# Reordered expert tiles, mask additions and ending in a fused attention and mixture-of-experts block

## The chip, the cores and the metric

The kernel runs on one core of a Trainium2 chip. The metric is the device time of one launch in microseconds (us). The core has five engines that run side by side, each with an instruction stream of its own: TensorE (PE) for matrix products, VectorE (DVE), ScalarE (ACT) and GpSimd (POOL) for the rest of the arithmetic, and SyncE (SP), which here only issues transfers. The engines wait for one another through semaphores. Data lies in SBUF (128 partitions); products are accumulated in PSUM.

## The reference

The input `query` has 2048 rows of 512. With xn = layernorm(query), the output is query + attention(xn) + experts(xn), all in float32.

```python
# attention: 16 heads, each with two score maps of width 16
q, k = rotary(xn @ Wq), rotary(xn @ Wk)
v = xn @ Wv                                    # 16 heads of 32
a1 = softmax(causal(q1 @ k1.T * 16 ** -0.5)) @ v
a2 = softmax(causal(q2 @ k2.T * 16 ** -0.5)) @ v
d = irfft((rfft(a1) - lam * rfft(a2)) * filt)  # along time, filt a Gaussian
attention = rmsnorm(d, over=32) * rms_weight * (1 - LAMBDA_INIT) @ Wout
# experts: 8 of inner width 352, the top 2 of each row; one shared of 704
s, e = top2(softmax(xn @ gate.T)); s = s / sum(s)
routed = sum_k s_k * ((silu(xn @ w1[e_k]) * (xn @ w3[e_k])) @ w2[e_k])
experts = routed + (silu(xn @ sw1) * (xn @ sw3)) @ sw2
```

## The kernel before

The rows are 16 tiles of 128 (`NT`), in 4 chunks of 512 (`QC`). Heads are worked in 8 pairs g. The order of PE, DVE, ACT, POOL and, in the middle part, SP is that in which the program issues instructions (`manual_schedule`).

**Start, up to about 250 us.** Layer norm, values, router, the list of slots for the routed rows, and the projections of queries and keys, which go out to memory.

**Middle, to about 1241 us.** The list `stream` holds the attention as 544 units: for each pair g and chunk qc from 3 down to 0, blocks of keys `kb`. A unit's `scores` (L822) puts transposed scores in PSUM, ACT takes the exponential into a tile `pt` (L835), and in the diagonal blocks POOL zeroes what lies beyond the diagonal with an `affine_select` (L840). Units with such blocks are called masked. `values` (L862) multiplies `pt` with v on PE, and `added` adds `pt` into `sum` on DVE (L876, L879). When a chunk is complete, `sums` (L888), `finish` (L900 to L908: `rcp`, `o_n`) and `put` (L917) turn it into the normalised difference in `vd`. When a pair is complete, `folded` (L928 to L970) does the sixteen-tile part of the filter's Fourier transform; POOL takes it in steps between other work, and the last pair is folded on DVE.

Between the attention units runs the generator `experts()`. It first does the shared expert for tiles that were left, then 34 tiles (`NR`) of routed rows. The first 28 (`NP`) hold 128 rows of one expert; each of the last 6 holds 64 rows of each of two experts. One tile goes through `xh` and `xg` (L180: products with the up weights `wu`), `xtanh` (DVE L191, L197), a transpose `ps_u` (PE L206) and its copies `uT` (DVE L208, L209), `xy` (L216: product with the down weights `wd`), `y_sb` (ACT L225) and a store to the array `ys` (SP L228). The weights have two buffers, `w_sb[0]` and `w_sb[1]`, each with a `wu` of 1408 KB and a `wd` of 768 KB. A single-expert tile uses one of them, a two-expert tile both. SP fetches `wu` (L146) into a buffer when `xg` has left it, and `wd` (L149) after `xy`. These stand behind the loads of queries `qS` and keys `kS` (L739) and the stores of `ys` in SP's queue. The rows of a tile, `xrow`, come by an indirect transfer that POOL issues (L623). PSUM tiles of `xh`, `xg`, `xy`, `ps_sum`, `ps_u`, `ps_ot`, `ps_st` share a pool of three buffers.

The units are taken in groups of four. A group issues the scores of its first two, the values of the group before, `sums` of a closing chunk, the other two scores, `finish`, and then the additions and one or more pieces of `experts()`:

```python
added(before)
added(u for u in units[:2] if not masked(u))
later = [u for u in units[2:] if not masked(u)]
while True:
    work()
    ...
added(later)
added(u for u in units if masked(u))
```

**Ending, from about 1241 us.** The shared expert of the last tile (`kept`; products `wh` L246 through the function `several`, its gate `ws` on ACT L256 and DVE L257 to L263), the convolution products of the filter (`ps_r`, `ps_z`, L1141), and then eight pairs of tiles: `y` (L1163), squares (ACT L1219), means (L1223, L1224), scale `a` (L1234), transposes `ps_tr` (L1262), the projection `po` (L1270), the addition to the residual `res` (L1275) and the store (L1276). `Pair`, `prepared`, `across`, `projected` and `finished` are these steps. Beside it, `res` is put together: SP loads 12 of the 16 tiles of `query` (L1120), POOL adds the shared expert's rows to them (L1123) and two gathers of `ys` (L1125), each a transfer that accumulates; the last four tiles follow in `still`, when buffers come free.

Of the kernel before, what the change touches and what calls it, by code (L numbers as in the profile page):

```python
# [8 lines left out]
F32 = mybir.dt.float32  # L9
# [4 lines left out]
ALU = mybir.AluOpType  # L14
# [31 lines left out]
NR = NS - 2  # L46

NP = (T * TOP // HALF - NX) // 2
WUP = NE * 2 * FI
WCOL = WUP + NF * E  # L50
CONVS = 23
# [16 lines left out]
def block_kernel(  # L68
# [527 lines left out]
    def middle(general):  # L596


        with ExitStack() as pools:
# [29 lines left out]
            def experts():  # L629
# [7 lines left out]
                for t0 in range(EARLY, NT - 1, TQ):  # L637
                    t1 = min(t0 + TQ, NT - 1)
                    last = t1 == NT - 1
                    cols = slice(t0 * P, t1 * P)  # L640
                    for n, us in enumerate(chunks(xnT[:, :, cols], u_last)):
                        if last and n == 0:
                            who_sb = mp.tile([P, E], F32, tag="x", name="who_sb")
                            who_sb = who_sb[:NR].rearrange("n (k p o) -> n k p o", k=TOP, o=2)
                            for k in range(TOP):
                                nc.sync.dma_start(who_sb[:, k], who[k][: NR * P, :].rearrange("(n p) o -> n p o", p=P))
                        elif last and n == 2:
                            nc.vector.tensor_add(who_sb[:, 0], who_sb[:, 0], who_sb[:, 1])
                        elif last and n == 3:
                            ps = bank([P, 2, NR], "ps_w")  # L650
                            for i in range(2):
                                nc.tensor.transpose(ps[:, i, :], who_sb[:, 0, :, i], ident[:NR, :NR])
                            nc.vector.tensor_copy(tok, ps[:, 0, :])
                            nc.vector.tensor_copy(wcol, ps[:, 1, :])
                        elif last and n == 5:


                            xr = [rows_of(0), rows_of(1)]
                            es = [routed(0)]
                            fetch_up(es[0], 0, nc.sync)  # L660
                        yield 3.45 * (t1 - t0) / TQ
                    if last:
                        es.append(routed(2))
                        fetch_up(es[1], 1, nc.sync)
                    for t in range(t0, t1):
                        y = result(us, t - t0, range(NF))
                        yield 2.6
                        stored(result(us, t - t0, range(NF, SCH), y), ysh[t], 0.5)
                        yield 2.6
# [5 lines left out]
                xT, late = transposed(xr.pop(0)), None  # L675
                yield 0.6

                sets = [[j] if j < NP else [2 * j - NP, 2 * j - NP + 1] for j in range(NR)]
                halves = [2 * j + i for j in range(NR) for i in range(len(sets[j]))]

                def places(j, part):
                    return [w_sb[n % 2][part] for n in sets[j]]

                def tile_down(j, uT):
                    return places(j, 1), uT, ys[j * P : (j + 1) * P, :], wcol[:, j : j + 1]

                for j in range(NR):
                    if j > 0:
                        late = tile_down(j - 1, turned_back(u))
                    half = up_first(places(j, 0), xT)  # L690
                    yield 2.9 if late else 2.4
                    u = up_third(places(j, 0), xT, half)
                    if j + 2 < NR:
                        xr.append(rows_of(j + 2))
                    for n in sets[j]:

                        m = n + 2 - len(halves)
                        es.append(routed(halves[n + 2]) if m < 0 else wex[NX + m : NX + m + 1])
                        fetch_up(es[n + 2], n % 2, nc.sync)
                    yield 2.4  # L700
                    if j + 1 < NR:
                        xT = transposed(xr.pop(0))
                    if late:
                        down(*late)
                        for n in sets[j - 1]:
                            fetch_down(es[n + 2], n % 2, nc.sync)
                    if j == 1:
                        shared.append(True)
                    if late:
                        yield 3.2  # L710
# [46 lines left out]
            def greatest(g, qc):  # L757
# [28 lines left out]
                nc.vector.tensor_copy(shift, ps.rearrange("p t q -> p (t q)"))  # L786
                return shift

            class Chunk:


# [19 lines left out]
                def scores(self, unit):  # L811
# [21 lines left out]
                    pt = pp.tile([P, 2, QC], F32, tag="pt", name="pt")  # L833
                    used = slice(min(c for *_, c, _ in unit), max(c + w for *_, c, w in unit))
                    nc.scalar.activation(pt[:, :, used], ps[:, :, used], AF.Exp, scale=SCALE)  # L835
                    for _, kb, _, col, _ in unit:
                        if kb >= qc * TQ and not general:

                            part = pt[:, :, col : col + P]
                            nc.gpsimd.affine_select(  # L840
                                out=part, in_=part, pattern=[[0, 2], [1, P]], compare_op=ALU.is_ge, fill=0.0,
                                base=0, channel_multiplier=-1,
                            )
                    ready = []
                    for h, kb, off, col, w in unit:
# [168 lines left out]
                nonlocal worked  # L1014
                worked += next(ex, work_all)

            def masked(entry):
                _, c, unit = entry
                return any(kb >= c.qc * TQ for _, kb, *_ in unit)

            def added(entries):

                for n, c, unit in entries:
# [5 lines left out]
            for i in range(0, len(stream), 4):  # L1029
# [19 lines left out]
                    c.finish()  # L1049
                held, before = [], held  # L1050
                added(before)
                added(u for u in units[:2] if not masked(u))
                later = [u for u in units[2:] if not masked(u)]
                while True:
                    work()
                    added(later[:1])
# [1 line left out]
                    if worked / (work_all - left) >= (i + 4) / len(stream):  # L1058
                        break
                added(later)  # L1060
                added(u for u in units if masked(u))
                if any(map(masked, units)) or not shared:
                    steps = 0
                else:
                    steps = 1 if any(map(masked, stream[i + 4 : i + 8])) else 2
                for _ in range(steps):
                    if folding is None and ready:
                        folding = folded(ready.pop(0), nc.gpsimd)
# [22 lines left out]
    def ending():  # L1091

        with tc.tile_pool(name="tail1", bufs=1) as t1, tc.tile_pool(name="tail", bufs=2) as tp, tc.tile_pool(
            name="tail_ps", bufs=4, space=PSUM
        ) as fps, tc.tile_pool(name="conv_ps", bufs=2, space=PSUM) as zps, tc.manual_schedule(
            engines={mybir.EngineType.PE, mybir.EngineType.DVE, mybir.EngineType.Activation, mybir.EngineType.Pool}
        ):
            conv = t1.tile([P, CONVS * P], F32, name="conv")  # L1100
            nc.scalar.dma_start(conv[:, : 11 * P], conv_t[:, : 11 * P])
            nc.scalar.dma_start(conv[:, 11 * P :], conv_t[:, 11 * P :])
            _, _, _, _, (_, _, stored), _ = expert(tp, fps)
            hidden, gated, times, _, result = shared_expert(tp, fps, 2)
            fetch_down(wex[NX + 1 : NX + 2], 1, nc.scalar)
            wo_sb = t1.tile([P, NE, E], F32, name="wo_sb")
            nc.scalar.dma_start(wo_sb, wout.rearrange("(c p) e -> p c e", p=P))
# [42 lines left out]
                return z  # L1150

            def copied(z):
                diff = tp.tile([P, 2, E], F32, tag="diff", name="diff")
                nc.scalar.copy(diff, z)
                return diff

# [23 lines left out]
            zr = pair("ps_r")  # L1180
            product(zr[:, 0, :], [(0, vd[:, 0, :])])
            product(zr[:, 1, :], [(1, vd[:, 1, :])])
            first = tp.tile([P, E], F32, tag="first", name="first", bufs=1)
            nc.scalar.copy(first, zr[:, 1, :])
            z4 = at(0, fold, 2)
            nc.vector.tensor_add(low[:, 0], zr[:, 0, :], first)
# [52 lines left out]
            def prepared(n):  # L1239

                z, i, by = ((z0, 0, 1.0), (z1, 2, ROOT), (z0, 1, COS8), (z1, 3, COS8 * ROOT))[n // 2]
                if n == 2:
                    nc.vector.tensor_sub(u0, u0, v0)
                    turned(z1, u0)
                elif n == 4:
                    nc.vector.tensor_sub(dv, zw, dv)
                    scaled(v1[:, 0], dv[:, 1], TAN8, dv[:, 0])
                    scaled(v1[:, 1], dv[:, 0], -TAN8, dv[:, 1])

                    nc.vector.tensor_add(z0[:, 0], u1[:, 0], v1[:, 1])  # L1250
                    nc.vector.tensor_sub(z0[:, 1], u1[:, 1], v1[:, 0])
                elif n == 6:
                    nc.vector.tensor_sub(u1[:, 0], u1[:, 0], v1[:, 1])
                    nc.vector.tensor_add(u1[:, 1], u1[:, 1], v1[:, 0])
                    turned(z1, u1)
                return Pair(z, i, by if n % 2 == 0 else -by)
# [55 lines left out]
            for n in range(NT // 2):  # L1312
# [3 lines left out]
                    pairs[n + 1].scales()  # L1316
                if n == 1:
                    stored(y, ysh[NT - 1], 0.5)
                if n + 1 < NT // 2:
                    aT = across(2 * n + 2)  # L1320
                if n + 2 < NT // 2:
                    pairs.append(prepared(n + 2))
                if ahead is not None:
                    finished(2 * n - 1, ahead)
                    still(2 * n - 1)
                if n + 2 < NT // 2:
                    pairs[n + 2].means()
                if n + 1 < NT // 2:
                    now, po = po, projected(after)
                    finished(2 * n, now)  # L1330
                    still(2 * n)
            finished(NT - 2, po)
            last(NT - 1, after)

# [135 lines left out]
```

## Time and profile before

| | |
|---|---|
| median of 3 runs | 1358.39 us (1357.41 to 1359.54) |
| profiled execution, its own time | 1360.14 us |
| its span | 1358.3 us |
| granted PE clock, mean | 0.994 |
| PE busy | 1312.6 us, 97% |
| DVE, ACT, POOL busy | 1005.4, 688.4, 626.3 us |
| bytes moved by DMA | 214.29 MB, mean 158 GB/s |

The span runs from the first to the last instruction or transfer of the profiled execution; the execution's own time is 1.8 us longer. Busy times count arithmetic, not the issuing of transfers. A number in brackets behind a row of a timeline is the idle time of the engine just before it and what ended that idle time; a wait for several things is put down to the one that came last. In a row, `xy<-wd,uT 128*64 128x512` is a product into `xy` from `wd` and `uT`, the stationary part of 128 by 64, the moving one of 128 by 512. A group of several records has the mark x and their number.

### The profile page before, as it was taken

How to read it: one execution, taken by the hardware profiler on the slowest of the kernel's cores; microseconds unless marked ns; L12 is line 12 of the kernel's file. 1: busy time of each engine (PE TensorE's matmuls, PEld its weight loads, DVE VectorE, ACT ScalarE, POOL GpSimd, SP SyncE). 2: the span in 40 equal slices, each digit the busy share in tenths (PEclk: the TensorE clock that was granted, in tenths of full speed). 3: DMA queues.
4: the chain of work that ended last, by engine and by line, in shares of the span. 5: the costliest groups of instructions: out<-in, count | busy, mean ns of one | idle time of the engine just before them, and what ended most of it. 6: DMA issues, size and time to landing. Idle time of an engine off the chain costs nothing.

```text
span 1358.3 us, 20810 instructions
## 1 busy us (share of the span) xinstructions
PE 1312.6 (97%) x7554; PEld 600.3 (44%) x7554; DVE 1005.4 (74%) x1344; ACT 688.4 (51%) x847; POOL 626.3 (46%) x671
## 2 busy tenths in 40 slices
PE   7999999999999999999999999899999999987998
PEld 3444444334443444445444444344544444443544
DVE  7049883287668778868889986778898788764785
ACT  2311110265656566676666666566676666640221
POOL 0002330012221323235968984778589469421764
PEclk9999999999999999999999999999999999998999
DMA  9406673200211122235665656555565666777997
GB/s 375 171 16 171 201 196 97 89 15 32 75 43 31 40 75 82 74 123 170 190 194 143 226 176 180 181 173 174 185 194 178 210 189 230 262 294 293 175 219 169
DMA packets 75578, 214.29 MB, mean 158 GB/s; under 512 B 12244, under 2 KB 12696, under 8 KB 69576
## 3 DMA queue, kind: packets, MB, share of 16 engines
q1 hardware_dynamic: 62744, 185.68, 41.7%
q0 software_dynamic: 11056, 22.78, 8.6%
q10 hardware_dynamic: 1664, 4.38, 0.9%
q8 instruction: 63, 1.03, 0.3%
q14 instruction: 51, 0.42, 0.1%
HBM read 169.69 MB, written 43.10 MB: 157 GB/s over the span
## 4 chain that ended last, share of the span: by engine, by line
PE 65%; DVE 6%; POOL 5%; DMA 3%; issue 1%; ACT 1%; SPq 0%; DVEq 0%; ACTq 0%; POOLq 0%
PE ps_o L862 16%; PE ps_s L822 12%; PE wh L246 8%; PE xy L216 6%; PE xg L180 5%; PE xh L180 5%; PE wy L284 4%; PE ps_sum L888 2%; DMA wu<-in_wex_dram 2%; POOL pt L840 1%; PE po L1270 1%; DMA wd<-in_wex_dram 1%; DVE sum L879 1%; PE ps_ot L900 1%; PE ps_x L165 1%
## 5 line engine op out<-in xcount | busy, mean ns | idle before, releaser
L879 DVE TENSOR_TENSOR sum<-sum,pt 128x1024 f32<-128x1024 f32 (+3 forms) x576 | 621.4, 1128 | 36.3 <-ACT pt L835 21.6
L835 ACT ACTIVATE pt<-ps_s 128x1024 f32<-128x1024 f32 x544 | 527.3, 1023 | 184.3 <-PE ps_s L822 131.0
L840 POOL TENSOR_SCALAR_AFFINE_SELECT pt<-pt 128x256 f32<-128x256 f32 x256 | 171.0, 693 | 358.7 <-ACT pt L835 357.5
L862 PE MATMUL ps_o<-pt,vd 128*32 128x512 f32 (+3 forms) x2560 | 268.0, 534 | 4.1 <-POOL pt L840 4.1
L822 PE MATMUL ps_s<-qS,kS 64*128 64x512 f32 (+3 forms) x1280 | 203.8, 406 | 2.0 <-DVEq L1335 1.6
L822 PEld LDWEIGHTS ps_s<-qS,kS 64*128 64x128 f32 x1280 | 97.1, 185 | 177.0 <-issue 95.9
L246 PE MATMUL wh<-xnT,wu 128*128 128x512 f32 (+1 forms) x352 | 150.4, 574 | 0.0
L862 PEld LDWEIGHTS ps_o<-pt,vd 128*32 128x32 f32 x2560 | 66.9, 109 | 125.8 <-issue 103.5
L545 PE MATMUL ps_x<-xnT,wqk_sb 128*128 128x512 f32 x256 | 110.5, 593 | 0.0
L498 POOL DMA_INDIRECT who<-pairs,slot x32 | 33.1, 1034 | 165.9 <-DVE pairs L495 104.9
L216 PE MATMUL xy<-wd,uT 128*128 128x512 f32 (+3 forms) x240 | 97.1, 606 | 7.7 <-DVE rcp L903 6.3
L246 PEld LDWEIGHTS wh<-xnT,wu 128*128 128x128 f32 x352 | 64.1, 190 | 72.7 <-issue 56.5
L180 PE MATMUL xh<-wu,xT 128*128 128x352 f32 (+1 forms) x320 | 90.5, 473 | 4.2 <-DMA wu<-in_wex_dram 3.3
L917 POOL TENSOR_TENSOR vd<-o_n 128x128 f32<-128x128 f32 x60 | 62.2, 1057 | 65.6 <-DVE o_n L908 65.5
L180 PE MATMUL xg<-wu,xT 128*128 128x352 f32 (+1 forms) x320 | 88.6, 468 | 0.0
L545 PEld LDWEIGHTS ps_x<-xnT,wqk_sb 128*128 128x128 f32 x256 | 48.4, 190 | 60.6 <-issue 60.6
L284 PE MATMUL wy<-wd,ws 128*128 128x512 f32 x160 | 74.8, 603 | 0.0
L257 DVE SCALAR_TENSOR_TENSOR ws<-ws,wh 128x512 f32<-128x512 f32 (+4 forms) x26 | 16.7, 644 | 73.6 <-ACT ws L256 73.6
L1125 POOL DMA_INDIRECT res<-ys,slot x32 | 54.9, 1715 | 25.3 <-DMA res<-ysh 13.5
L562 ACT CAST hi<-turned 128x1024 fp32r<-128x1024 f32 x16 | 16.7, 1045 | 93.9 <-DVE turned L560 70.9
L180 PEld LDWEIGHTS xh<-wu,xT 128*128 128x128 f32 (+1 forms) x320 | 48.0, 176 | 31.7 <-issue 6.5
L180 PEld LDWEIGHTS xg<-wu,xT 128*128 128x128 f32 (+1 forms) x320 | 46.6, 174 | 34.4 <-issue 14.8
(254 smaller groups left out, 1416.8 us busy)
## 6 DMA issues: line engine op xcount, KB each, us to landing
wu<-in_wex_dram SPq DMA_DIRECT2D x44, 1408.0 KB
wd<-in_wex_dram SPq DMA_DIRECT2D x43, 768.0 KB
kS<-parts_k SPq DMA_DIRECT2D x128, 128.0 KB
qS<-parts_q SPq DMA_DIRECT2D x256, 64.0 KB
ys<-y_sb SPq DMA_DIRECT2D x34, 256.0 KB
parts_q<-hi SPq DMA_DIRECT2D x32, 256.0 KB
parts_k<-hi SPq DMA_DIRECT2D x16, 256.0 KB
parts_k<-turned SPq DMA_DIRECT2D x16, 256.0 KB
```

The source lines that it names most:

```text
L180: nc.tensor.matmul(dst[r, :], xT[:, c, r], w[:, o : o + FI], start=(c == 0), stop=(c == NE - 1), skip_group_check=True,)
L216: nc.tensor.matmul(y[r, :], uT[:m, ic, r], w[:m, ic * E : (ic + 1) * E], start=(ic == 0), stop=(ic == NF - 1), skip_group_check=True,)
L246: nc.tensor.matmul(dst, w_sb[o // WUP][0][:, o % WUP : o % WUP + P], x[:, c, :], start=(c == 0), stop=(c == NE - 1))
L284: nc.tensor.matmul(y, us[i][:, t * P : (t + 1) * P], w_sb[i // NF][1][:, i % NF * E : (i % NF + 1) * E], start=(i == 0), stop=(i == SCH - 1),)
L545: nc.tensor.matmul(ps[:, i, :], wqk_sb[st, qk][:, i, c, :], xnT[:, c, cols], start=(c == 0), stop=(c == NE - 1),)
L822: nc.tensor.matmul(to, k, queries[2 * g + h, qc][r, off : off + w], start=True, stop=not general)
L835: nc.scalar.activation(pt[:, :, used], ps[:, :, used], AF.Exp, scale=SCALE)
L840: nc.gpsimd.affine_select(out=part, in_=part, pattern=[[0, 2], [1, P]], compare_op=ALU.is_ge, fill=0.0, base=0, channel_multiplier=-1,)
L862: nc.tensor.matmul(self.o[r : r + 32, off:], vd[:, kb, v0 : v0 + 32], pt[:, s, :], start=first, stop=self.ended, skip_group_check=True,)
L879: nc.vector.tensor_add(to, to, pt)
L917: eng.tensor_add(vd[:, self.qc * TQ : (self.qc + 1) * TQ, v0 : v0 + 32], self.o_n[:, :, h, 0, :], self.o_n[:, :, h, 1, :],)
L1125: nc.gpsimd.indirect_dma_start(out=came[k], out_offset=None, in_=ys, in_offset=bass.IndirectOffsetOnAxis(ap=slot[:, step - 2, order[k] : o ...
```

## The change

1. The tiles are worked in the order of a list `ORDER`: the 26 first single-expert tiles, the 6 two-expert tiles, and then the last two single-expert tiles. Which weights are requested when follows from that list, the shared expert's for the ending among them.
2. The additions of a group's first two units all stand before the work of `experts()`, masked ones too. Those of the other two stand as before.
3. The unit that holds block d+2 of both heads gets one `affine_select` over both, 128x4x128, in place of two of 128x2x128.
4. Before a group with masked units, a step of `folded` is issued only if another pair waits to be folded or the last pair is at work; otherwise none.
5. In the ending, `ws`, `first` and `diff` come from a pool of their own (`tail2`). The shared expert's output of the last tile is scaled on ACT instead of DVE. The addition to `res` of each odd tile stands before the next pair's transposes and `prepared`, and that of each even tile before the next pair's means. The preparation of pair 4 is split over pairs 3 and 4.

```diff
+ORDER = [*range(NP - 2), *range(NP, NR), *range(NP - 2, NP)]
...
-                            xr = [rows_of(0), rows_of(1)]
-                            es = [routed(0)]
+                            xr = [rows_of(j) for j in ORDER[:2]]
+                            es = [routed(2 * ORDER[0])]
...
-                        es.append(routed(2))
+                        es.append(routed(2 * ORDER[1]))
...
-                sets = [[j] if j < NP else [2 * j - NP, 2 * j - NP + 1] for j in range(NR)]
-                halves = [2 * j + i for j in range(NR) for i in range(len(sets[j]))]
+                sets, halves = [], []
+                for tj in ORDER:
+                    n = 1 if tj < NP else 2
+                    sets.append(range(len(halves), len(halves) + n))
+                    halves += [2 * tj + i for i in range(n)]
...
-                    return places(j, 1), uT, ys[j * P : (j + 1) * P, :], wcol[:, j : j + 1]
+                    tj = ORDER[j]
+                    return places(j, 1), uT, ys[tj * P : (tj + 1) * P, :], wcol[:, tj : tj + 1]
...
-                        xr.append(rows_of(j + 2))
+                        xr.append(rows_of(ORDER[j + 2]))
...
+            def masked(chunk, unit):
+                return any(kb >= chunk.qc * TQ for _, kb, *_ in unit)
...
-                    for _, kb, _, col, _ in unit:
-                        if kb >= qc * TQ and not general:
-
-                            part = pt[:, :, col : col + P]
+                    if masked(self, unit) and not general:
+
+                        cols = [col for *_, col, _ in unit]
+                        if cols == [0, 2 * P]:
+                            chosen = [pt.rearrange("p s (h q) -> p (s h) q", h=2)[:, :, :P]]
+                        else:
+                            chosen = [pt[:, :, col : col + P] for col in cols]
+                        for part in chosen:
                             nc.gpsimd.affine_select(
-                                out=part, in_=part, pattern=[[0, 2], [1, P]], compare_op=ALU.is_ge, fill=0.0,
-                                base=0, channel_multiplier=-1,
+                                out=part, in_=part, pattern=[[0, part.shape[1]], [1, P]], compare_op=ALU.is_ge,
+                                fill=0.0, base=0, channel_multiplier=-1,
                             )
...
-                added(u for u in units[:2] if not masked(u))
-                later = [u for u in units[2:] if not masked(u)]
+                added(units[:2])
+                later = [u for u in units[2:] if not masked(*u[1:])]
...
-                added(u for u in units if masked(u))
-                if any(map(masked, units)) or not shared:
+                added(u for u in units[2:] if masked(*u[1:]))
+                if any(masked(*u[1:]) for u in units) or not shared:
                     steps = 0
+                elif any(masked(*u[1:]) for u in stream[i + 4 : i + 8]):
+                    steps = 1 if ready or units[0][1].g == NG - 1 else 0
                 else:
-                    steps = 1 if any(map(masked, stream[i + 4 : i + 8])) else 2
+                    steps = 2
...
-        with tc.tile_pool(name="tail1", bufs=1) as t1, tc.tile_pool(name="tail", bufs=2) as tp, tc.tile_pool(
-            name="tail_ps", bufs=4, space=PSUM
-        ) as fps, tc.tile_pool(name="conv_ps", bufs=2, space=PSUM) as zps, tc.manual_schedule(
+        with tc.tile_pool(name="tail1", bufs=1) as t1, tc.tile_pool(name="tail2", bufs=2) as t2, tc.tile_pool(
+            name="tail", bufs=2
+        ) as tp, tc.tile_pool(name="tail_ps", bufs=4, space=PSUM) as fps, tc.tile_pool(
+            name="conv_ps", bufs=2, space=PSUM
+        ) as zps, tc.manual_schedule(
...
-            _, _, _, _, (_, _, stored), _ = expert(tp, fps)
-            hidden, gated, times, _, result = shared_expert(tp, fps, 2)
+            _, _, _, _, (_, _, stored), _ = expert(tp, fps, by_scalar=True)
+            hidden, gated, times, _, result = shared_expert(t2, fps, 2)
...
-                diff = tp.tile([P, 2, E], F32, tag="diff", name="diff")
+                diff = t2.tile([P, 2, E], F32, tag="diff", name="diff")
...
-            first = tp.tile([P, E], F32, tag="first", name="first", bufs=1)
+            first = t2.tile([P, E], F32, tag="first", name="first", bufs=1)
...
-                elif n == 4:
+                elif n == 3:
                     nc.vector.tensor_sub(dv, zw, dv)
                     scaled(v1[:, 0], dv[:, 1], TAN8, dv[:, 0])
                     scaled(v1[:, 1], dv[:, 0], -TAN8, dv[:, 1])
+                elif n == 4:
...
+                if ahead is not None:
+                    finished(2 * n - 1, ahead)
+                    still(2 * n - 1)
                 if n + 1 < NT // 2:
                     aT = across(2 * n + 2)
                 if n + 2 < NT // 2:
                     pairs.append(prepared(n + 2))
-                if ahead is not None:
-                    finished(2 * n - 1, ahead)
-                    still(2 * n - 1)
-                if n + 2 < NT // 2:
-                    pairs[n + 2].means()
                 if n + 1 < NT // 2:
                     now, po = po, projected(after)
                     finished(2 * n, now)
                     still(2 * n)
+                if n + 2 < NT // 2:
+                    pairs[n + 2].means()
```

## The prediction

> **What bounds the kernel now.** I read the busy shares first. These lines are the head of the page (us, share of the span, number of instructions):
>
> ```profile
> PE 1312.6 (97%) x7554; PEld 600.3 (44%) x7554; DVE 1005.4 (74%) x1344; ACT 688.4 (51%) x847; POOL 626.3 (46%) x671
> ```
>
> TensorE (PE) is busy 97% of the span, and the change leaves its products the same in number. So it can gain only what PE spends waiting, or running slowly just after a wait. The list of waits on PE (waiting instruction, what released it: total us, times, longest) says where the waits are:
>
> ```profile
> PE xy L216 <- DVE rcp L903: 6.3, 4, 3.3
> PE ps_o L862 <- POOL pt L840: 4.1, 4, 1.6
> PE xh L180 <- DMA wu<-in_wex_dram: 3.3, 2, 2.7
> PE ps_tr L1262 <- DVE a L1234: 2.7, 3, 1.3
> PE ps_z L1141 <- DVE vd L1187: 2.6, 1, 2.6
> PE wh L246 <- DMA wu<-in_wex_dram: 2.3, 1, 2.3
> PE po L1270 <- DVE res L1275: 2.1, 2, 1.9
> ```
>
> The largest, 7.3 us at the start, is not touched and not shown. Next I read the timeline of PE over the last routed tiles (start, duration, group, count, idle before it):
>
> ```profile
> 1195.28 4.27 PE L180 MATMUL xh<-wu,xT 128*64 128x352 f32 x14 [2.67 <-DMA wu<-in_wex_dram]
> ...
> 1202.66 2.59 PE L180 MATMUL xg<-wu,xT 128*64 128x352 f32 x16
> ...
> 1230.42 5.26 PE L246 MATMUL wh<-kept,wu 128*128 128x128 f32 x32 [2.34 <-DMA wu<-in_wex_dram]
> 1236.39 1.04 PE L216 MATMUL xy<-wd,uT 128*64 128x512 f32 x2 [0.70 <-DVE vd L966]
> 1238.16 2.79 PE L216 MATMUL xy<-wd,uT 128*64 128x512 f32 x10 [0.73 <-DMA wd<-in_wex_dram]
> 1241.78 1.98 PE L1141 MATMUL ps_r<-vd,conv 128*128 128x512 f32 x4 [0.83 <-ACT y_sb L225]
> ...
> 1249.75 0.67 PE L1141 MATMUL ps_z<-xnT,conv 128*128 128x512 f32 x1 [2.55 <-DVE vd L1187]
> ```
>
> A wait costs more than its bracket. The 14 products after the 2.67 us wait take 4.27 us, where 16 of the same kind take 2.59, so 14 should take 2.27. The windows of 20 us give PE a granted clock of 0.91 in 1180-1200, 1220-1240 and 1240-1260, and 1.00 in 1200-1220.
>
> Last, the waits that start the ending: ScalarE's timeline, then the queue of SyncE (SP), then the first and last gathers of GpSimd (POOL).
>
> ```profile
> 1247.12 0.38 ACT L256 ACTIVATE ws<-wh 128x256 f32<-128x256 f32 x1 [5.39 <-DMA ys<-y_sb]
> ```
> ```profile
> 1247.16 7.25 SPq L1120 DMA_DIRECT2D res<-in_query_dram  x12
> ```
> ```profile
> 1260.42 1.64 POOL L1125 DMA_INDIRECT res<-ys,slot  x1 [4.10 <-DMA res<-ysh]
> ...
> 1345.97 1.54 POOL L1125 DMA_INDIRECT res<-ys,slot  x1 [2.00 <-DMA res<-ys,slot]
> ```
>
> ACT and SP both start at 1247.1, when the last tile's store `ys<-y_sb` has landed. From there a second chain runs beside PE: loads of `res`, then gathers on POOL. Its last gather starts at 1345.97. By the view of tile `res`, these transfers take 5.1 us or more to land, so it lands at 1351.07 at the earliest; the first of the last two additions on DVE starts at 1351.43, released by PE. Chain and PE end almost together; the shorter of their two gains is what the end can gain.
>
> **What the Trainium skill says.** "TensorE: Matmul & The Clock Gate", section "Part 1: The HAM clock gate", says that a clock gate halves the PE clock after an idle window of about 3.4 us, and frees it after about as long a time of work. The trace agrees in kind (4.27 against 2.27 us), though here waits of 2.3 to 2.7 us already do it. "SBUF — State Buffer", section "Who interferes with whom", says that a VectorE operation with two SBUF inputs and a GpSimd one that reads SBUF shut each other out. The trace agrees: one sum addition at 846.76 takes 3.52 us instead of 1.2 while POOL folds, and one 128x128 step of POOL (L947) takes 4.31 us, another (L951) 0.46. "DMA: Bandwidth & Descriptors", section "Issuing engines are not separate DMA queues", says that transfers issued by different engines share the same 16 DMA engines. In the trace the DMA share is 0.69 to 0.76 in 1160-1240 and 0.91 to 1.09 in 1240-1320: moving an issue to another engine creates no bandwidth.
>
> **The change part by part.** Times are against the profiled span of 1358.3 us (execution 1360.14 us). The median of the runs is 1358.39 us. I subtract my saving from the median.
>
> *1. Order of tiles.* A tile of two experts needs 2.88 MB of `wu` (2 halves) and gives about 10 us between the end of its xg, which frees the buffers, and the next xh. At the five places where another weight load must follow one of these tiles, three gaps of 9.9 to 10.1 us sufficed. One of 9.7 us did not: SP issued only at 1183.28, behind a query load, and the weights landed 12.0 us later. A single-expert tile needs one half, and earlier gaps between such tiles are 11.6 and 13.5 us. With singles last, the shared expert's weights are also requested one tile earlier; the order of PE puts 7 of its 16 products (`wh<-kept`, two records each) ahead of the last xy, 9 behind. What goes:
> - xh at 1195.28: 2.67 + (4.27 - 2.27) = 4.67
> - xh at 1216.87: 0.68
> - wh at 1230.42: 2.34 + (5.26 - 3.58) = 4.02; 3.58 is what the chain of waits gives 32 such records at 1273.22
> - xy: 0.70 + 0.73 waiting; the 12 took 3.83 and take 2.80 elsewhere, 1.03; together 2.46
> - ps_r's wait for ACT, 0.83, now beneath the nine wh products
>
> The sum is **12.7 us**. The products on the path are the same: the two-expert tile's xy takes 2.80 us, the single's 2.74. SP's order moves too: the `rw` loads stand ahead of a store, and one `wd` of 768 KB (half of a pair that took 8.5 us) is fetched once more. That transfer lies among attention work, before the last tile; I price it at nothing, and up to 4.2 us if the last `wd` comes to be waited for. Bounds: 8 (one 4.67 stall comes back at a new place) to 14.
>
> *2. Masked additions first.* The wait of 3.27 us for rcp at 854.49 is the one to read. PE's xy needs a PSUM bank that rcp and o_n release. On DVE ahead of rcp:
>
> ```profile
> 845.63 0.53 DVE L197 TENSOR_TENSOR xtanh<-xg,xtanh 128x352 f32<-128x352 f32 x1 [2.84 <-PE xg L180]
> 846.07 0.69 DVE L876 COPY sum<-pt 128x1024 f32<-128x1024 f32 x1
> 846.67 7.59 DVE L879 TENSOR_TENSOR sum<-sum,pt 128x768 f32<-128x768 f32 x6
> ```
>
> DVE idles 2.84 us and then does six additions. Two units' additions now come before L197 and fill that idle time, so rcp comes about 2.4 us sooner; the six xy behind it took 4.54 us, half of a warm twelve is 1.4, so I count 1.5 of that excess. That is 3.9. The other three waits for rcp total 3.0, say 1 goes. What is added: on DVE these additions now wait for POOL's selects with uT (L208, L209) and xtanh (L191, L197) queued behind them, and PE's ps_u, xy and next xh wait for those. I put 1.5 against it. Net **-3.4**, from -8 to +4.
>
> *3. One select for two heads* gives 224 instead of 256 on POOL (mean 693 ns). The unit's additions needed both halves anyway. POOL is 46% busy; nothing, or 0.4 us on the four waits. *4. Fewer fold steps* before a masked group: by the order of instructions the folds move only from the fifth on, after about 905 us. POOL's waits at 757 and 882 (1.58, 1.4) stay, the 0.84 at 1119 may go: **-0.6**. The folds are needed only at the end, where the last pair is folded on DVE; bounds 0.8 either way. The middle is together -4.
>
> *5. The ending.* ws, first and diff leave the zone of the pool that waits for the store. ACT's L256 then no longer waits 5.39 us, so first (1247.40) and vd L1187 come over 2.55 us sooner: PE's ps_z loses its wait and the slow run behind it (15.67 us for the 32, against 14.4): 3.8. DVE's residual addition moves ahead of y and the reduce, so po's waits go (2.1). The output store's scaling, 0.68 us, moves from DVE to ACT, and one of ps_tr's waits for a goes (1.27). DVE does 17 to 18 us of work in each 20 here, so nothing more. PE's end: 12.7 + 3.8 + 3.4 = 19.9 us sooner.
>
> But `res` still waits for the last store of ys, which follows the last xy. That comes 12.7 - 0.83 + 2.0 (nine wh products, 9/16 of 3.58, now behind it) = 13.9 us sooner, and POOL's 24 gathers at 1.86 us each do not shorten. The transfers of the shared weights have left that stretch, so I allow the chain 1.1 more: the end gains **15**, with 13 and 19.9 as bounds.
>
> Total: 15 + 4 = 19; 1358.39 - 19 = **1339.4 us**.
>
> **The rivals.**
> - *PE sets the end.* If `res` runs ahead, the end gains 19.9, with the middle 24: 1334.5; with its full 8, 1330.5. For it: the gathers' waits were longest while the DMA share was above 0.9. Against: 24 issues on POOL are bound by issue, not by bandwidth.
> - *The middle gives nothing or loses.* DVE waits for selects that stand behind POOL's folds: +0 to +4 at 32 masked groups of about 0.1 us: 1343 to 1347. For it: the 4.31 us step. Against: POOL's selects near 841 to 845 end about when DVE has nothing to do.
> - *Slower: the weight waits move with the tiles.* If the load takes longer than the 10 us gap at each of the five places, five stalls of 4.67 us cost 23.3 against 19 gained: 1362.7. It turns at 19/4.67, so above four stalls, and when the landing takes over 10 us. Against: three of five fitted in a stretch with a DMA share above 0.69, and now come earlier.
> - *Nothing moves*, because another wait ends last where the bracket names one: 1358.
>
> **How the numbers follow.** Chances: residual chain 0.50; PE sets the end 0.22; middle gives nothing 0.22; nothing moves 0.02; slower 0.04. The range 1329 to 1350 runs from the full gain of both to an end of -13 with a middle of +4, a little wider for the unpriced transfer. A change of 0.2%, 2.7 us, is about what can be measured. Faster 0.94, same 0.02, slower 0.04.
>
> **What would show it.** In the profile after: no wait above 1 us of xh, wh or xy for wu or wd after 1150; the first `ws` on ACT directly behind its products; `res` loads about 14 us earlier; the last additions on DVE waiting for gathers, not for PE (if for PE, the first rival). The longest wait of xy for rcp should be under 1.5 us. A stall at each two-expert tile, or more waits of ps_u and xy for DVE, would make the prediction wrong.

## The result, and the profile after

The changed kernel's median is 1349.69 us (1348.36 to 1351.29, 4 runs) against 1358.83 us for the kernel before (4 runs of this series); the ratio is 0.9925, 95% interval 0.9904 to 0.9947. A second series gave 0.9898 (0.9872 to 0.9924). That is some 9 to 14 us faster, where 19 were forecast. The profiled execution has a span of 1347.3 us (its own time 1349.09). The head of the page after:

```profile
PE 1310.0 (97%) x7554; PEld 599.2 (44%) x7554; DVE 1014.1 (75%) x1343; ACT 689.5 (51%) x848; POOL 612.7 (45%) x639
```

The waits on PE, in the columns of before (lines are those of the changed file: xh is L182, rcp L916, po L1284):

```profile
PE xh L182 <- DMA wu<-in_wex_dram: 7.8, 4, 3.1
PE ps_tv L378 <- DVE xn_all L365: 7.3, 1, 7.3
PE ps_tr L1276 <- DVE a L1247: 5.4, 5, 1.7
...
PE ps_o L875 <- POOL pt L853: 1.9, 3, 1.4
...
PE ps_z L1154 <- DVE vd L1200: 1.0, 1, 1.0
PE xy L218 <- DVE rcp L916: 0.8, 1, 0.8
```

The wait for rcp fell from 6.3 to 0.8 us, POOL's from 4.1 to 1.9, and the waits of po and wh are gone. But xh now waits 7.8 us for weights, where it waited 3.3. PE's timeline shows where:

```profile
1074.85 2.58 PE L182 MATMUL xh<-wu,xT 128*64 128x352 f32 x14 [1.49 <-DMA wu<-in_wex_dram]
...
1099.71 1.40 PE L182 MATMUL xh<-wu,xT 128*64 128x352 f32 x2 [3.06 <-DMA wu<-in_wex_dram]
1102.94 4.96 PE L182 MATMUL xh<-wu,xT 128*64 128x352 f32 x14 [1.83 <-DMA wu<-in_wex_dram]
...
1162.90 2.58 PE L182 MATMUL xh<-wu,xT 128*64 128x352 f32 x14 [1.40 <-DMA wu<-in_wex_dram]
```

These four waits stand at three of the six two-expert tiles at their new places: one at the first, two at the second (its first two products wait for one half of the weights, the other fourteen for the other) and one at the fifth. To see what each stretch gained, set the two timelines of PE beside each other at the same work: at the start of the first `ps_sum` product of the chunk that comes up at that time.

| work | before, us | after, us | shift |
|---|---|---|---|
| a chunk in the shared expert's time | 621.12 | 622.12 | +1.0 |
| after POOL's wait near 757 | 791.77 | 790.72 | -1.1 |
| after the rcp wait near 854 | 861.36 | 855.02 | -6.3 |
| ahead of the two-expert tile with the long wait | 1098.43 | 1093.91 | -4.5 |
| behind it | 1153.37 | 1157.94 | +4.6 |
| next chunk | 1189.04 | 1195.43 | +6.4 |
| first `ps_r` | 1241.78 | 1232.92 | -8.9 |
| end of the last product | 1353.12 | 1341.33 | -11.8 |

The first row is not put down to the change: the same 1.0 us stands at 325 us already and stays as it is up to 621 us, and the profiles of experiments 1, 4 and 12, which run the same instructions there, lie between 1.2 us ahead of the kernel before and 1.8 us behind it. From it the reading of this profile is: additions and POOL's waits, 7.3 us gained; two-expert tiles at the new places, 10.9 us lost between 1098 and 1189; the last tiles, 15.3 us gained between 1189 and ps_r; the ending, 2.9 us gained. Experiment 12 shows how far a second profile of the same kernel departs from it.

The ending starts as forecast. ACT's first `ws` no longer waits for the store, and SP's loads of `res` come 9.3 us sooner (1237.89 against 1247.16):

```profile
1233.17 0.38 ACT L258 ACTIVATE ws<-wh 128x256 f32<-128x256 f32 x1 [1.32 <-PE wh L248]
```
```profile
1237.89 7.12 SPq L1133 DMA_DIRECT2D res<-in_query_dram  x12
```

The last additions on DVE wait for gathers, but PE's last product ends only 0.4 us ahead of the row's start:

```profile
1339.16 0.69 DVE L1289 TENSOR_TENSOR res<-res,po 128x512 f32<-128x512 f32 x1 [4.42 <-DMA res<-ys,slot]
1341.75 0.75 DVE L1300 TENSOR_TENSOR res<-res,po 128x256 f32<-128x256 f32 x2 [1.91 <-DMA res<-ys,slot]
```

### The profile page after: what moved, and what is told of

Read it like the earlier page. It is cut to its first block, busy times and chain, and to the rows that moved or that the text cites. A ratio compares the mean times of both kernels' runs of the same rounds, so it can differ in the third digit from the quotient of the medians.

```text
span 1347.3 us, 20781 instructions
## 1 busy us (share of the span) xinstructions
PE 1310.0 (97%) x7554; PEld 599.2 (44%) x7554; DVE 1014.1 (75%) x1343; ACT 689.5 (51%) x848; POOL 612.7 (45%) x639
## 4 chain that ended last, share of the span: by engine, by line
PE 60%; POOL 9%; DMA 7%; issue 2%; DVE 2%; ACT 0%; SPq 0%; POOLq 0%; DVEq 0%; ACTq 0%
PE ps_o L875 16%; PE ps_s L831 11%; PE wh L248 8%; PE xy L218 5%; PE xh L182 5%; PE xg L182 5%; PE wy L286 4%; DMA wu<-in_wex_dram 3%; POOL res L1138 3%; DMA res<-ysh 2%; PE ps_sum L901 1%; POOL pt L853 1%; DVE sum L892 1%; PE ps_x L167 1%; PE ps_ot L913 1%
## 5 line engine op out<-in xcount | busy, mean ns | idle before, releaser
L892 DVE TENSOR_TENSOR sum<-sum,pt 128x1024 f32<-128x1024 f32 (+2 forms) x576 | 629.5, 1142 | 30.5 <-POOL pt L853 13.6
L853 POOL TENSOR_SCALAR_AFFINE_SELECT pt<-pt 128x256 f32<-128x256 f32 (+1 forms) x224 | 163.2, 750 | 388.0 <-ACT pt L844 362.5
L182 PE MATMUL xh<-wu,xT 128*128 128x352 f32 (+1 forms) x320 | 93.7, 480 | 8.6 <-DMA wu<-in_wex_dram 7.8
L182 PE MATMUL xg<-wu,xT 128*128 128x352 f32 (+1 forms) x320 | 88.6, 468 | 0.0
L930 POOL TENSOR_TENSOR vd<-o_n 128x128 f32<-128x128 f32 x60 | 59.0, 1002 | 53.8 <-DVE o_n L921 53.7
L182 PEld LDWEIGHTS xh<-wu,xT 128*128 128x128 f32 (+1 forms) x320 | 48.4, 178 | 38.9 <-DMA wu<-in_wex_dram 8.2
L182 PEld LDWEIGHTS xg<-wu,xT 128*128 128x128 f32 (+1 forms) x320 | 46.6, 174 | 34.3 <-issue 14.8
L382 PE MATMUL ps_tv<-wv_sb,xnT 128*128 128x512 f32 x128 | 59.3, 616 | 0.7 <-ACT xnT L379 0.7
```

The source lines that it names most:

```text
L182: nc.tensor.matmul(dst[r, :], xT[:, c, r], w[:, o : o + FI], start=(c == 0), stop=(c == NE - 1), skip_group_check=True,)
L382: nc.tensor.matmul(pv, xnT[:, c, t * P : (t + 1) * P], wv_sb[:, c, :], start=(c == 0), stop=(c == NE - 1))
L853: nc.gpsimd.affine_select(out=part, in_=part, pattern=[[0, part.shape[1]], [1, P]], compare_op=ALU.is_ge, fill=0.0, base=0, channel_multip ...
L892: nc.vector.tensor_add(to, to, pt)
```

## The experiments

Theory A: the order took the waits at the end away and set new ones at 1070 to 1165. Rival B: the order kept its full gain, and the masked additions lost the rest on DVE. Each kernel was timed against the kernel before. Experiments 1 to 4, 5 to 8 and 9 to 11 each share a chip, so across these groups the ratios are compared, not the microseconds.

**1. The order undone.** `ORDER = [*range(NR)]` in the changed kernel.

> The changed kernel with the tiles in their old order (two-expert tiles last); everything else as changed. Theory A (the order took waits for weights away at the end, but put new ones of about 10 us where the two-expert tiles now stand, at 1070 to 1165): the new waits go, the old ones at 1180 to 1240 return, net 3 to 5 us slower than the changed kernel, about 1353. Rival B (the order kept its full gain of 12 to 13 us and the missing 10 us were lost by the masked additions on DVE): 12 us slower, about 1362, and the loss in the middle stays.

1349.31 us, ratio 0.9914 (0.9900 to 0.9929): level with the changed kernel, against both numbers. Where the waits stand is as A has it. Between 1098 and 1189 the shift now stays flat (-6.5 to -6.6 us), and PE's timeline has the old waits at the end:

```profile
1188.31 4.14 PE L182 MATMUL xh<-wu,xT 128*64 128x352 f32 x14 [2.33 <-DMA wu<-in_wex_dram]
...
1223.15 3.84 PE L248 MATMUL wh<-kept,wu 128*128 128x128 f32 x32 [2.42 <-DMA wu<-in_wex_dram]
```

B falls. The order, beside the other parts, brought about nothing in net that the times can tell.

**2. Two-expert and single tiles by turns.** `ORDER = [*range(NP - 6), *(t for k in range(6) for t in (NP + k, NP - 6 + k))]`.

> The changed kernel with two-expert and single-expert tiles by turns over the last 12 places. Theory A: the load of two halves falls behind a tile that needs one, so the waits of xh for wu in the middle (7.8 us and the slow products behind them, about 11 in all) mostly go: 6 to 10 us faster than the changed kernel, about 1342. Rival B: no difference, within 1 us. A third reading (C: a two-expert tile waits wherever it stands, since its 2.9 MB never land within the gap): no faster than 1349, with about as many waits at other times.

1380.70 us, ratio 1.0142 (1.0121 to 1.0163): slower than the kernel before by 19 us. C's bound (no faster than 1349) holds, but its reason was in none of the three readings: it is `wd` for which PE now waits most, 23.8 us in 3 waits. See experiment 8.

**3. The masked additions back.** `added(u for u in units[:2] if not masked(*u[1:]))`, and `added(u for u in units if masked(*u[1:]))` at the end.

> The changed kernel with the masked additions of the first two units back behind the work of the experts. Theory A: the wait of xy for rcp near 850 returns, 4 to 6 us slower, about 1354. Rival B: faster by several us, since DVE no longer waits for POOL's selects ahead of the experts' copies.

1355.56 us, ratio 0.9967 (0.9954 to 0.9981), by the ratios some 6 to 9 us slower than the changed kernel in its two series. Its waits on PE:

```profile
PE xy L218 <- DVE rcp L916: 7.4, 4, 3.7
...
PE xh L182 <- DVE uT L210: 4.0, 1, 4.0
```

**4. The ending undone.** The function `ending` of before, unaltered, in the changed kernel.

> The changed kernel with the ending of the kernel before (pools and order). Theory A: the ending kept about 4 of the 7 us forecast for it, because DVE's work and the residual chain hold the tail: 4 us slower, about 1353.5, with the 5.4 us wait of ACT for the store of ys and the wait of ps_z back. Rival D (the residual chain alone sets the end, and it is the same in both): within 1.5 us of the changed kernel.

1350.32 us, ratio 0.9927 (0.9910 to 0.9943): in time not to be told from the changed kernel. Its profile has from ps_r to the end of PE's last product 111.4 us (1231.32 to 1342.75), as before (111.3); the changed kernel has 108.4 and experiment 1 has 108.1. So the ending is worth 3 us of PE's time in profiles, within what the times leave open. Of the two forecasts D's number came true, but not its reason: in this profile DVE's last additions wait for PE, not for gathers. ACT waits as before:

```profile
1236.79 0.38 ACT L258 ACTIVATE ws<-wh 128x256 f32<-128x256 f32 x1 [6.54 <-DMA ys<-y_sb]
```

**5. The additions alone.** Part 2 in the kernel before.

> The kernel before with part 2 alone: the masked additions of a group's first two units ahead of the experts' work. Theory A2 (formed from the first four runs: this part is most of the gain, and the order and the ending each bring about nothing): 6 to 8 us faster than before, about 1352.5, with the waits of xy for rcp and of ps_o for POOL near 757 and 850 gone. Rival: 3 us or less, if the gain needs the other parts beside it.

1352.29 against 1359.67 us, ratio 0.9946 (0.9932 to 0.9959): 7.4 us faster. This part carries most of the change. The waits for rcp fall to 0.5 us in all; POOL's are 3.1 instead of 4.1.

**6. Parts 3 and 4 undone.** The loop with one select per block, and `steps = 1 if any(masked(...)) else 2`.

> The changed kernel with two selects and the old rule for fold steps (parts 3 and 4 undone). Theory A2: both are hidden, within 1.5 us of the changed kernel. Rival E (they removed POOL's waits, so part of the middle's gain is theirs): 2 to 4 us slower, with the wait near 757 back.

1349.42 us, ratio 0.9927 (0.9901 to 0.9954): level with the changed kernel, as far as an interval of some 3.6 us to either side can tell. The gain between 735 and 791 us stays, so it is not theirs.

**7. No loads for the last head pair.** In `load_keys` and `load_queries`, for `g == NG - 1`: `keys[h, c] = keys[h - 2, c]`, `queries[h, qc] = queries[h - 2, 0]`.

> The changed kernel without the key and query loads of the last head pair (it reads the pair before; those 48 transfers are left out). Theory F (the weights of two-expert tiles land late because the loads of keys and queries for the last pair share SP's queue and the DMA engines with them): the waits of xh for wu at 1070 to 1165 fall from 7.8 us to under 2, 7 to 11 us faster, about 1340. Rival G (2.9 MB simply take longer than the gap, whatever stands beside them): the waits stay above 5 us, under 3 us faster.

1340.10 us, ratio 0.9847 (0.9828 to 0.9866), some 7 to 11 us faster than the changed kernel. Of the 7.8 us this is left:

```profile
PE xh L182 <- DMA wu<-in_wex_dram: 1.2, 1, 1.2
```

So the weights at the first two of the three tiles are late because of the loads of keys and queries beside them; the wait that is left stands at the fifth two-expert tile. In the changed kernel, SP issues four key loads at 1077.85, and then weights and queries in this order:

```profile
1083.21 3.09 SPq L148 DMA_DIRECT2D wu<-in_wex_dram  x2
1086.34 16.87 SPq L745 DMA_DIRECT2D qS<-parts_q  x8
```

SP issues the weights at once when xg has left the buffers (its last product ends at 1083.2), so it is not the queue that holds them back. Going by the products that wait for them, they come 16 and 20 us after the first issue. The DMA view of 1077 to 1083, where only loads of keys and queries are issued (40 equal slices, busy tenths and rate, then the issues):

```profile
DMA  1111110101441030001111111111111111111111
GB/s 55 41 55 41 41 55 27 41 0 41 164 164 68 0 27 0 0 27 55 55 55 41 41 55 55 55 55 41 55 41 41 55 41 55 41 41 55 55 41 41
...
kS<-parts_k SPq DMA_DIRECT2D x4, 128.0 KB
qS<-parts_q SPq DMA_DIRECT2D x1, 64.0 KB
```

A busy share of 0.1 at 41 to 55 GB/s is about two of 16 engines at work. Where no such load is under way (1155.5 to 1164.5, weights for the most part), 402 GB/s pass. Early in the kernel before, the two kinds of load can be seen apart, first queries alone (302 to 304 us), then keys alone (309 to 318 us):

```profile
DMA packets 177, 0.25 MB, mean 125 GB/s; under 512 B 55, under 2 KB 55, under 8 KB 177
q1 hardware_dynamic: 177, 0.25, 52.0%
qS<-parts_q SPq DMA_DIRECT2D x2, 64.0 KB
```
```profile
DMA packets 214, 0.43 MB, mean 47 GB/s; under 512 B 6, under 2 KB 6, under 8 KB 214
q1 hardware_dynamic: 214, 0.43, 13.1%
kS<-parts_k SPq DMA_DIRECT2D x1, 128.0 KB
```

52% of 16 engines is 8 of them, 13% is 2. So the slow loads are those of keys, and queries (32 partitions each) are not slow by themselves. The key loads fill 64 partitions and read one source for both halves of them; which of the two confines them to two engines was not separated.

**8. One two-expert tile in each long turn.** Two-expert tiles at the places 2, 9, 15, 22, 28, 30.

> The changed kernel with the two-expert tiles at the places 2, 9, 15, 22, 28 and 30 of 34, that is one in each long turn (qc = 3), between two bursts of query and key loads. Theory F: no wait of xh or xy for weights over 1.5 us, 6 to 10 us faster than the changed kernel, about 1341. Rival G: each of the six places has its stall of 2 to 5 us, 1350 to 1370, as with tiles by turns.

1395.00 us, ratio 1.0262 (1.0238 to 1.0286): the forecast failed, and the rival's range was passed too. xh waits 17.4 us for wu (4 times) and xy 22.1 us for wd (3). SP's queue before one of them, and PE's row:

```profile
789.28 8.27 SPq L747 DMA_DIRECT2D qS<-parts_q  x8
797.59 2.26 SPq L735 DMA_DIRECT2D kS<-parts_k  x4
799.96 0.48 SPq L232 DMA_DIRECT2D ys<-y_sb  x1
800.69 2.18 SPq L153 DMA_DIRECT2D wd<-in_wex_dram  x1
```
```profile
817.38 5.38 PE L220 MATMUL xy<-wd,uT 128*64 128x512 f32 x10 [8.34 <-DMA wd<-in_wex_dram]
```

Twelve loads stand ahead of `wd`, the four of keys last; it lands 16.7 us after its issue. All three `wd` that PE waits for here, and the two longest of experiment 2, were issued behind four key loads in this way and came 14 to 18 us later. Places meant to be clear of such loads at xh were not clear at xy, one tile later. One of the three waits here (3.6 us) and one in experiment 2 (5.1 us) is a single-expert tile's; why the two-expert tiles are hit harder was not traced further.

**9. One transfer for each load.** From the traces came F2: these loads are slow by their form, 32 or 64 partitions each. (The views under experiment 7 confine that to the keys.) Keys and queries are stored as four parts, in the order of the tiles' partitions (48 stores more), and each head's tile is one transfer:

```diff
-                for part, src in ((0, hi.bitcast(F32)), (1, o), (2, hi.bitcast(F32)))[: 3 - qk]:
+                for part, src in enumerate((big, o, big, o) if qk else (big, o, o, big)):
...
+                    src = parts[0][2 * h : 2 * h + 2, :, :, qc * QC : (qc + 1) * QC].rearrange("s a d t -> (s a d) t")
+                    nc.sync.dma_start(q.bitcast(F32), src)
```

> The changed kernel with keys and queries kept in memory in the layout of the tiles, so that each load is one transfer of 128 partitions (4 per turn) in place of 12 of 32 or 64; 48 more stores of 256 KB in the first 250 us. Theory F2 (formed from the traces: those loads run at about 50 GB/s with a DMA share of 0.1, that is on one or two of the 16 DMA engines, and the part of the weights that goes through the same engines queues behind them): the loads run several times faster, the waits of xh for wu at 1070 to 1165 go, 7 to 10 us faster after 250 us; the added stores may cost 0 to 6 us before it. 1340 to 1346. Rival H (the loads are slow because their rows lie apart in memory, or the wait is one of SP's queue alone): the rate stays near 50 GB/s and so do the waits; 1349 or more.

1341.31 us, ratio 0.9866 (0.9848 to 0.9884): faster than the kernel before and, by the ratios, some 4 to 8 us faster than the changed kernel (the interval of its second series overlaps this one a little). The waits of xh for wu are 1.5 us, and a turn's query loads, the ones behind the pair of `wu`, hold SP's queue for 1.84 us instead of 16.87:

```profile
1086.77 1.77 SPq L148 DMA_DIRECT2D wu<-in_wex_dram  x2
1088.59 1.84 SPq L740 DMA_DIRECT2D qS<-parts_q  x2
```

In a stretch that holds the same turn's loads and one `wd` (1076 to 1083) 2.01 MB pass at a mean of 287 GB/s. The rows of a load lie as far apart in memory as before, so that part of H falls. The page "SBUF — State Buffer" of the Trainium skill, section "Can I just issue two DMAs to hit both halves?", states that only a transfer that spans all 128 partitions reaches all ports, and that transfers cannot be fused. The query loads alone agree with it (52% of the engines' time at 32 partitions each); that key loads come to 13% does not follow from it. What was varied is the form of both kinds of load at once, which also cut their number on SP from 12 to 4 a turn; the number of engines that carried each one is worked out from the busy share, not seen. In its profile 6.5 us are lost before 325 us, in that of experiment 10, with the same start, 0.6.

**10. The same with the old order.**

> The same with the tiles in the old order, two-expert tiles last. Theory F2: the order is worth its forecast once nothing stands in the way of the weights: 6 to 12 us slower than with the new order, with the waits for wu near 1185 and for wh near 1223 still there. Rival: the order is worth nothing here either, within 2 us.

1351.56 us, ratio 0.9949 (0.9932 to 0.9966). Against experiment 9, on the same chip, the order is now worth 0.0083 of 1358 us, that is 11.3 us (the forecast was 6 to 12), with an uncertainty of some 3.5 (the two half-widths of 0.0018 joined). The waits at the end are there:

```profile
PE xh L182 <- DMA wu<-in_wex_dram: 3.4, 2, 2.3
...
PE wh L248 <- DMA wu<-in_wex_dram: 2.0, 1, 2.0
```

**11. A shorter residual chain.** `for step in range(3)` in `still`.

> The changed kernel without the second gather of the last four tiles (4 of POOL's 32 gathers; that part of the sum is left out). If the residual chain set the end by more than a little, as the prediction took it: 2 us or more faster. If PE and DVE set it, as the trace of the changed kernel has it (PE's last product ends at 1341.3, the last addition at 1342.5): under 1.3 us.

1346.78 us, ratio 0.9895 (0.9874 to 0.9915). Not decided by time: experiment 12 has the same level. In its profile PE's last product ends at 1341.69, and DVE then waits for PE instead of gathers. PE's end did not come sooner, so the chain cost the changed kernel's profile 1 us at most.

**12. The changed kernel again.**

> The changed kernel once more, to see how far its ratio to the kernel before and the places of its waits repeat. If its level is that of the first runs: ratio 0.990 to 0.995, with waits of xh for wu of 5 us or more in all between 1070 and 1165. If the run without the last gathers (ratio 0.9895) was faster only because runs differ: 0.989 to 0.992, overlapping it; if the last gathers cost some 4 us: clearly above it, 0.992 or more.

1347.74 us (1341.81 to 1352.01), ratio 0.9898 (0.9872 to 0.9924), with 7.2 us of waits of xh for wu. The waits stand at the same tiles; the runs spread over 10 us. This profile has one more wait, which the first profile of the same kernel lacks:

```profile
844.85 1.24 PE L831 MATMUL ps_s<-qS,kS 64*128 64x512 f32 x3 [1.01 <-DMA qS<-parts_q]
846.32 0.46 PE L831 MATMUL ps_s<-qS,kS 64*128 64x512 f32 x1 [0.23 <-DMA qS<-parts_q]
```

With the 32 slower products behind it (3.78 us, against 2.36 in the first profile) it leaves 4.6 us of the 7.3 that the first profile gained up to 861 us. The profiles of experiments 2, 4, 6 and 7 have this wait too, of 1.8 to 3.7 us; those of 9 and 10, with the whole loads, do not. So the loads cost the changed kernel time in a second place, in some executions only; it may be part of the spread of the runs, which was not tested.

## Why the prediction was right or wrong

The direction was right, the saving was about half of the forecast (about two thirds in the second series), and the step that failed is part 1: it put nothing for weight waits at the new places. The total is at the slow end of the range of 1329 to 1350 and came there by luck: part 1 gave about nothing for 12.7 us forecast, and part 2 twice its forecast.

- **Part 1, the order: 12.7 us forecast.** The removals were there and somewhat larger, 15.3 us between 1189 and ps_r. The failed term is the price of the new places: nothing, with one returning stall of 4.67 us as the bound. The sign that it named, no wait above 1 us for weights after 1150, did not come either (1.40 at 1162.90). There were four waits at three tiles, three of them and 10.9 us between 1098 and 1189 alone; experiment 1 puts the net at about zero. The argument "three of five gaps of 10 us sufficed" carried over gaps from a stretch after the last pair's key loads. The old place was sheltered: there, no keys of a next pair are loaded, only queries. The prediction named the mechanism as its slower rival (at all five transitions, 23.3 us) and refused it on the DMA share; about half of it came true, at three places instead of five. The share, a mean over 16 engines, hides two busy ones: 13% was all that the key loads showed. Experiments 7, 9 and 10 show the rest: without those loads most of the waits go (7), and with the loads in another form the order is worth 11.3 us (9 against 10), near its forecast.
- **Part 2, the additions: 3.4 forecast, 7.3 measured** in the first profile (4.6 in that of experiment 12, with its wait for queries), 7.4 by experiment 5. The chain to rcp was read rightly. Of the waits for rcp 5.5 us went, not 3.3 + 1. POOL's wait near 757, which the prediction left standing as one behind folds, fell from 1.9 us in two waits to 0.2; it goes with the additions (experiments 3, 5 and 6), by which path stays open. The 1.5 us set against the part did not show.
- **Parts 3 and 4: 0.6 to 1 forecast, nothing that can be told** from the spread of the runs (experiment 6).
- **Part 5, the ending: 7.2 us of PE's time forecast, 2.9 measured.** ps_z's wait fell from 2.55 to 1.0 and the slower products behind it went (13.97 us for the 32 products, against 15.67); po's waits of 2.1 went. In exchange the waits of ps_tr for `a` rose from 2.7 to 5.4: DVE's additions came first and the scales later. The prediction counted one of the `a` waits as gone; the order of DVE's work moved the wait, it did not shorten the work.
- **The residual chain, as what sets the end,** is not confirmed: DVE does wait for gathers last, as forecast, but PE ends 1 us ahead (experiment 11). `res` came 9.3 us sooner, not 14, since the last xy itself ended only 9.9 us sooner.

The total by these steps, from the first profile: 1.0 start, -7.3 additions, +1.8 from 861 to 1098, +10.9, -15.3, -2.9, +0.8 from PE's end to the span's: -11.0, the difference of the spans.

## What to carry to other kernels

Before work is moved to another place, list what the same queue and the same engines carry at that place: transfers that keep only two engines busy hide in a mean busy share and still delay a wide one, here by 6 to 10 us. A gap that sufficed in one stretch is no measure for another with other loads. On an engine that works in order, putting what can already run ahead of what still waits is cheap and was worth more here than the larger rearrangement.

## What the runs showed of the hardware

Loads of keys (64 partitions by 2 KB, one source for both halves), alone, ran at 47 GB/s with a DMA share of 13%, the time of about 2 of 16 engines. Loads of queries (32 partitions by 2 KB), alone, ran at 125 GB/s with 52%, the time of 8. Two weight loads of 1.4 MB issued behind four such key loads took 16 and 20 us to land; the pair issued at 1114.04, behind none, was there for the product at 1124.17. Keys and queries in transfers of 128 partitions passed in a stretch of 287 GB/s.
